# Setup of a graph-attention kernel: the first eight loads ordered anew over two DMA queues, and three chunks of the neighbours' sums computed ahead of q's projection

## The chip, the cores and the metric

The kernel runs on one core of one Trainium2 chip. The metric is the device time of one execution in microseconds (us): 586.49 us in the median of three runs (586.25 to 587.98). The core's engines are named as the profile names them: PE is TensorE's matmul, PEld its weight load, DVE is VectorE, ACT is ScalarE, POOL is GpSimd, SP is SyncE, which here does nothing but issue transfers. A name with a q behind it (SPq, ACTq) is that engine's sequencer, from which a transfer (DMA) is issued.

## What is computed

One graph-attention layer over B = 16 graphs of N = 512 nodes with F = 512 features. Each node attends to the first NG = 20 nodes of its graph, in two directions d, with H = 16 heads of 32 features. Cut to what matters here:

```python
row_zero  = v.sum(-1) == 0                                  # (B, N)
q_exp     = where(row_zero, 0, q[:, None, :])               # q is (B, 512)
self_feat = concat([v, q_exp], -1) @ W_self.T + b_self      # (B, N, F)
output = self_feat
for d in range(2):
    A  = adj if d == 0 else swap(adj); A = A[:, :, :20, :]
    kv = self_feat[:, :20]
    qh, kh = self_feat @ Wq[d].T + bq[d], kv @ Wk[d].T + bk[d]
    aff = heads(qh) . heads(kh) / sqrt(32)
    aff = where(A.sum(-1) > 0, aff, NEG) + (A @ w_bias + b_bias)
    out_t = softmax(aff) @ kv                               # per head
    output += heads(out_t) @ Wout[d] + bout[d]
result = v + relu(output)
```

The first thing that all else needs is `self_feat` of the 20 neighbours of every graph, 16 * 20 = 320 columns: a product of their features with the first half of `W_self`, plus the product of q with the second half, the latter only where a node's features do not sum to zero.

## The kernel before, in words

The program is one function with its order of work written out by hand: each engine gets its instructions in the order in which the code names them, and waits where an operand isn't there yet. It has a setup (lines 458 to 764), in which the weights are loaded, the neighbours' features, keys and values are computed and the keys are folded into the score weights, and a loop over the 16 graphs (from line 786) with four tiles of 128 nodes each. The change touches the first 17 us of the setup alone.

Everything in the setup's beginning is cut into C = 4 chunks of 128 input features (the partitions):

- `xkv[:, k]`, 128 x 320, chunk k of the 320 neighbours' features (160 KB each); `ws_v[:, k]`, 128 x 512, chunk k of the half of `W_self` that multiplies them (256 KB each). The helper `kv_rows(k, queue)` (line 501) loads both: `xkv` always from SP's queue, `ws_v` from the queue given.
- `ws_q`, 128 x 4 x 512 (1024 KB), the half of `W_self` that multiplies q; `q_sb` (32 KB) is q itself.
- `bs_sb`, `bk_sb`: two small biases, needed by ACT at lines 579 and 592.

The loads stand at lines 506 to 528. ACT's queue issues `ws_v` chunks 0 and 1, `bs_sb`, `bk_sb`; SP's queue issues `xkv` chunks 0 and 1, `q_sb`, `ws_q`, then chunks 2 and 3 of `xkv` and `ws_v`, then the key weights `wk` (line 515, needed from line 586 on), the query weights `wq_sb`, a broadcast bias row, the first graph's `x` and so on.

The work on them, in PE's order:

1. seven matmuls on a tile of ones (line 496) that need no load;
2. `kv_terms(fc, k)` (line 536): for chunk k and each quarter fc of the output one fp32 matmul of 320 columns into the PSUM bank `kv_ps[fc]`; the profile shows each as two instructions. It runs for k = 0 and 1, that is 16 instructions;
3. q's projection (line 547): four matmuls into `ps_q`, one per chunk, eight instructions;
4. `kv_terms(fc, 2)`, eight instructions, while ACT copies q's projection from PSUM to `q4` (line 551);
5. the sum of the neighbours' features over all partitions (line 554, two instructions), from `rsk`, which POOL adds up from the four chunks of `xkv` (lines 531 to 533);
6. four matmuls of `q4` with a selecting matrix `sel` (line 559, eight instructions), which sum the four chunks' parts of q's projection and turn them; DVE copies the result to `qw` (line 563);
7. `kv_terms(fc, 3)`, eight instructions, beside which DVE and POOL form `qp`, DVE adds it to the finished bank (`kvn`, line 576) and ACT adds the bias (`kvT`, line 579);
8. `key_rows` (line 582), which needs `kvT` and `wk`, and from there the rest of the setup.

Of the kernel before, what the change touches and what calls it, by code (L numbers as in the profile page):

```python
# [13 lines left out]
P = 128  # L14
# [4 lines left out]
def gat_kernel(  # L19
# [20 lines left out]
    nc = tc.nc  # L40
    B, F, N = xT.shape
    NG, L = adj.shape[3], adj.shape[4]
    H, DH = 16, 32
    C = F // P
# [28 lines left out]
    ws_v = const.tile([P, C, F], F32, name="ws_v")  # L73
# [384 lines left out]
    with tc.tile_pool(name="setup", bufs=1) as sp, tc.tile_pool(name="ps_acc", bufs=4, space=PSUM) as acc["pool"]:  # L458
# [4 lines left out]
        q_sb = sp.tile([P, C, B], F32, name="q_sb")  # L463
# [10 lines left out]
        ws_q = load.tile([P, C, F], F32, tag="x", name="ws_q", bufs=3)  # L474
        wk_sb = [sfp.tile([P, C, F], F32, tag="sf", name=f"wk{d}") for d in range(2)]

        with tc.tile_pool(name="setup_k", bufs=1) as sk:
            xkv = sk.tile([P, C, BM], F32, name="xkv")
# [19 lines left out]
            def rows(sb, src, queue=nc.sync):  # L498
                queue.dma_start(sb, src.rearrange("(c p) f -> p c f", p=P))

            def kv_rows(k, queue=nc.sync):
                rows(xkv[:, k : k + 1], xkvT[bass.ts(k, P)])
                rows(ws_v[:, k : k + 1], wsT[bass.ts(k, P)], queue)


            kv_rows(0, nc.scalar)
            kv_rows(1, nc.scalar)
            nc.scalar.dma_start(bs_sb, b_self)
            nc.scalar.dma_start(bk_sb, bk)
            nc.sync.dma_start(q_sb, qT)  # L510
            rows(ws_q, wsT[F:])
            kv_rows(2)
            kv_rows(3)
            for d in range(2):
                rows(wk_sb[d], wkT[d])
            for d in range(2):
# [19 lines left out]
            def kv_terms(fc, k):  # L536
                nc.tensor.matmul(  # L537
                    kv_ps[fc][:, :BM], ws_v[:, k, bass.ts(fc, P)], xkv[:, k],
                    start=(k == 0), stop=(k == C - 1),
                )  # L540

            for k in range(2):
                for fc in range(C):
                    kv_terms(fc, k)

# [3 lines left out]
                )  # L549
            q4 = sk.tile([P, F], F32, name="q4")  # L550
            nc.scalar.copy(q4, ps_q[:, 0])
            for fc in range(C):
                kv_terms(fc, 2)
            nc.tensor.matmul(ps_q[:, 1, :BM], ones, rsk, start=True, stop=True)
            nc.vector.tensor_scalar(nzk, ps_q[:, 1, :BM], 0.0, None, ALU.not_equal)

# [510 lines left out]
```

## Time and profile before

| | |
|---|---|
| median of three runs | 586.49 us |
| the profiled execution's own time | 586.05 us |
| its span from the first to the last instruction | 583.9 us |
| PE busy | 575.7 us, 99% of the span |
| DVE busy | 489.0 us, 84% |
| ACT busy | 395.6 us, 68% |
| POOL busy | 384.9 us, 66% |
| moved by DMA | 124.14 MB, mean 213 GB/s |

The profile is one execution; its times are counted from the first instruction. A busy PE is not PE at its peak: a matmul's record is stretched by the one ahead of it, so starts are better evidence than ends. In a row of the timeline stand the start, the duration, the engine, the line, the operation, the tile written and those read, the count, and in brackets how long the engine was idle before and what released it. In a row on issues stand the tile and its source, the queue, the count, the size and the time from issue to landing. The chain of waits gives start, duration and name of each piece of the path that ended last.

### The profile page before, as it was taken

The numbers are of one execution on the slowest core, as the hardware profiler recorded it, in microseconds if no ns is written. First come the engines' busy times: TensorE is split into PE (matmuls) and PEld (weight loads), VectorE is DVE, ScalarE is ACT, GpSimd is POOL, SyncE is SP. The second block draws the span as 40 slices with busy tenths as digits, with TensorE's granted clock in tenths as the row PEclk, the third lists the DMA queues.
The fourth block names the chain that finished last, engine by engine and source line by source line (L and its number), as shares of the span: only waits on it lengthen the run. The fifth ranks groups of instructions, "written<-read, shape, count | busy, mean of one in ns | idle before, by whom it ended". The sixth has DMA issues, their size and how long they took to land.

```text
span 583.9 us, 30310 instructions
## 1 busy us (share of the span) xinstructions
PE 575.7 (99%) x13184; PEld 437.0 (75%) x13184; DVE 489.0 (84%) x783; ACT 395.6 (68%) x1162; POOL 384.9 (66%) x351
## 2 busy tenths in 40 slices
PE   9999999999999999999999999999999999999996
PEld 6654547887878787877878787787887878787873
DVE  0485565889898989899999999898989898989895
ACT  1334644586877777868686868687786877777671
POOL 2405663648778685858586777686868677776775
PEclk9999999999999999999999999999999999999999
DMA  8999899857766675757576767676676765664404
GB/s 303 388 407 311 331 377 320 273 123 213 209 197 196 185 214 169 217 167 217 168 214 171 214 171 212 177 199 188 199 202 187 199 198 172 199 199 114 144 15 146
DMA packets 103220, 124.14 MB, mean 213 GB/s; under 512 B 21712, under 2 KB 71920, under 8 KB 101040
## 3 DMA queue, kind: packets, MB, share of 16 engines
q1 hardware_dynamic: 101296, 119.79, 66.8%
q8 instruction: 104, 1.70, 1.3%
q0 software_dynamic: 672, 1.36, 1.0%
q10 hardware_dynamic: 1120, 1.06, 0.5%
q14 instruction: 28, 0.23, 0.2%
HBM read 82.30 MB, written 40.24 MB: 210 GB/s over the span
## 4 chain that ended last, share of the span: by engine, by line
PE 98%; DVE 0%; issue 0%; ACT 0%; DVEq 0%
PE ps_s L365 46%; PE ps_a L282 17%; PE ps_c L282 9%; PE ps_o L435 6%; PE ps_d L282 4%; PE ps_v L649 3%; PE ps_k L586 3%; PE ps_sf L205 2%; PE ps_kv L537 2%; PE ps_o L779 1%; PE ps_warm L496 1%; PE ps_nz L189 0%; PE ps_s L354 0%; PE ps_c L622 0%; PE ps_q L547 0%
## 5 line engine op out<-in xcount | busy, mean ns | idle before, releaser
L365 PEld LDWEIGHTS ps_s<-g,sf 128*32 128x32 f32 x8192 | 262.8, 110 | 20.9 <-issue 13.0
L365 PE MATMUL ps_s<-g,sf 128*32 128x152 f32 x8192 | 276.7, 293 | 0.5 <-ACT st L689 0.5
L337 ACT COPY both<-add 32x80 f32<-32x80 f32 x512 | 130.8, 256 | 53.8 <-DVE add L328 48.0
L417 POOL TENSOR_TENSOR s<-s,sm 128x640 f32<-128x640 f32 x63 | 80.4, 1276 | 94.2 <-DVE sm L416 68.2
L344 POOL TENSOR_TENSOR full<-cq,both 128x640 f32<-128x640 f32 x64 | 100.4, 1568 | 27.5 <-issue 21.3
L317 ACT ACTIVATE prod<-adj,wb_sb 128x80 f32<-128x80 int32 x330 | 112.4, 433 | 0.0
L392 ACT ACTIVATE s<-s 128x640 f32<-128x640 f32 x63 | 46.5, 738 | 64.1 <-DVE s L387 63.8
L449 POOL TENSOR_TENSOR o<-o,x 128x512 f32<-128x512 f32 x60 | 76.4, 1297 | 0.0
L379 DVE TENSOR_TENSOR full<-ps_s,full 128x608 f32<-128x608 f32 x63 | 48.8, 774 | 27.9 <-PE ps_s L365 22.6
L415 DVE TENSOR_REDUCE sm<-s 128x32 f32<-128x640 f32 x63 | 50.8, 806 | 9.5 <-ACT s L392 9.2
L282 PE MATMUL ps_a<-t,ws_s 128*32 128x246 f32 x960 | 55.4, 370 | 0.0
L383 DVE TENSOR_REDUCE ps_s<-full 128x32 f32<-128x640 f32 x63 | 52.2, 828 | 2.2
L424 DVE STREAM_TRANSPOSE wt<-s 128x640 f32<-128x640 f32 x63 | 52.7, 837 | 0.6 <-POOL s L417 0.6
L387 DVE TENSOR_TENSOR s<-full,ps_s 128x640 f32<-128x640 f32 x63 | 51.5, 817 | 1.1
L282 PEld LDWEIGHTS ps_a<-t,ws_s 128*32 128x32 f32 x960 | 31.6, 110 | 16.0
L328 DVE TENSOR_REDUCE add<-prod 128x80 f32<-128x960 f32 x32 | 36.8, 1150 | 6.2 <-ACT prod L317 4.4
L247 POOL TENSOR_TENSOR t<-x 128x492 f32<-128x492 f32 x30 | 34.6, 1153 | 9.5 <-DVE ps_s L383 5.4
L446 ACT ACTIVATE o<-o,bo 128x512 f32<-128x512 f32 x60 | 38.3, 713 | 0.6 <-DVE o L444 0.6
L435 PE MATMUL ps_o<-wt,vd 32*32 32x512 f32 (+5 forms) x816 | 36.7, 578 | 0.0
L444 DVE TENSOR_TENSOR o<-ps_o,sf 128x512 f32<-128x512 f32 x60 | 36.7, 668 | 0.0
L289 DVE SCALAR_TENSOR_TENSOR u<-nz,qw,ps_a 128x246 f32<-128x246 f32 x90 | 36.6, 448 | 0.0
L247 POOL TENSOR_TENSOR t<-x,t 128x492 f32<-128x492 f32 x30 | 34.5, 1150 | 2.3 <-DMA x<-in_xT 1.1
(239 smaller groups left out, 719.5 us busy)
## 6 DMA issues: line engine op xcount, KB each, us to landing
g_d<-st SPq DMA_DIRECT2D x16, 1064.0 KB, 5.9
g<-g_d SPq DMA_DIRECT2D x56, 304.0 KB, 3.6
out_T<-o SPq DMA_DIRECT2D x60, 256.0 KB, 3.3
x<-in_xT SPq DMA_DIRECT2D x56, 256.0 KB, 3.2
xn<-in_xn SPq DMA_DIRECT2D x52, 256.0 KB, 3.3
adj<-in_adj SPq DMA_DIRECT2D x56, 220.0 KB, 3.2
nz<-nz_d SPq DMA_DIRECT2D x14, 256.0 KB, 4.6
wk<-in_wkT SPq DMA_DIRECT2D x2, 1024.0 KB, 7.7
```

The source lines that it names most:

```text
L247: done["xsum"] = nc.gpsimd.tensor_sub(t, one, two)
L282: nc.tensor.matmul(to, lhs, x[:, k], start=start, stop=stop, skip_group_check=n != 2)
L317: nc.scalar.activation(p[:, :, l], a[:, :, l], AF.Identity, scale=wb_sb[:, l : l + 1])
L337: nc.scalar.copy(adds[b, h][bass.ts(a, R), :, g], add[r].rearrange("p (t m) -> p t m", t=2))
L344: done["full"] = nc.gpsimd.tensor_add(f, cqs[b].unsqueeze(1).to_broadcast(shape), adds[b, nt // 2][:, nt % 2].unsqueeze(2).to_broadcast(sh ...
L365: nc.tensor.matmul(to, sfs[b][:, k, bass.ds(nt * P + (2 * g + j) * R, R)], of, start=(onto is None and k == 0 and (whole or j == 0)), stop ...
L383: nc.vector.tensor_reduce(mx, f, AX.X, ALU.max)
L387: done["weigh"] = nc.vector.tensor_sub(s, f, mx.unsqueeze(3).to_broadcast(full))
L417: done["normal"] = nc.gpsimd.tensor_mul(s, s, sm.unsqueeze(3).to_broadcast(full))
L424: nc.vector.transpose(wts[b][:, nt], s.rearrange("p a h m -> p (a h m)"))
L435: nc.tensor.matmul(banks[a][bass.ds(at // 2 * DH, n * DH)].rearrange("p (t n) -> p t n", n=32), vd[r, bass.ds(at * DH, n * DH)], wt[r, :, ...
L449: nc.gpsimd.tensor_add(o[:, c], o[:, c], xs[b][:, c])
```

## The change

The eight transfers that come first are others, and the queues of some are changed:

| place | before | after |
|---|---|---|
| SP's queue | `xkv` 0, `xkv` 1, `q_sb`, `ws_q`, `xkv` 2, `ws_v` 2, `xkv` 3, `ws_v` 3, then `wk` | `xkv` 0, `xkv` 1 to 3 as one transfer of 480 KB, `ws_v` 2, `ws_v` 3, then `wk` |
| ACT's queue | `ws_v` 0, `ws_v` 1, `bs_sb`, `bk_sb` | `ws_v` 0, `ws_v` 1, `ws_q`, `q_sb`, `bs_sb`, `bk_sb` |

On PE, `kv_terms` runs for k = 0, 1 and 2 ahead of q's projection; between the projection and the sum of features (item 5) no chunk is left.

```diff
             kv_rows(0, nc.scalar)
-            kv_rows(1, nc.scalar)
+            rows(xkv[:, 1:], xkvT[P:])
+            rows(ws_v[:, 1:2], wsT[P : 2 * P], nc.scalar)
+            for k in (2, 3):
+                rows(ws_v[:, k : k + 1], wsT[bass.ts(k, P)])
+            rows(ws_q, wsT[F:], nc.scalar)
+            nc.scalar.dma_start(q_sb, qT)
             nc.scalar.dma_start(bs_sb, b_self)
             nc.scalar.dma_start(bk_sb, bk)
-            nc.sync.dma_start(q_sb, qT)
-            rows(ws_q, wsT[F:])
-            kv_rows(2)
-            kv_rows(3)
             for d in range(2):
                 rows(wk_sb[d], wkT[d])
...
-            for k in range(2):
+            for k in range(C - 1):
                 for fc in range(C):
                     kv_terms(fc, k)
...
             nc.scalar.copy(q4, ps_q[:, 0])
-            for fc in range(C):
-                kv_terms(fc, 2)
             nc.tensor.matmul(ps_q[:, 1, :BM], ones, rsk, start=True, stop=True)
```

## The prediction, made before the changed kernel ran

> **What bounds the kernel now.** I read the page first, then the chain of waits over the first 20 us, then the issues and the timeline of that stretch.
>
> ```profile
> span 583.9 us, 30310 instructions
> PE 98%; DVE 0%; issue 0%; ACT 0%; DVEq 0%
> ```
>
> PE carries 98% of the chain that ended last, so whatever moves PE's work in the setup moves the end by the same amount unless some later wait takes it up. The chain over the stretch that the change touches:
>
> ```profile
> 1.04 3.36 PE ps_warm L496 x14
> 4.40 5.49 PE ps_kv L537 x16
> 9.89 0.98 PE ps_q L547 x8
> 10.87 2.35 PE ps_kv L537 x8
> 13.22 0.54 PE ps_q L554 x2
> 13.76 0.80 PE ps_q L559 x8
> 14.56 2.25 PE ps_kv L537 x8
> 16.81 3.28 PE ps_k L586 x11
> ```
>
> Every piece begins where the last one ended. From 1.04 us on there is no hole: no transfer holds PE up, neither chunk 1 nor `ws_q`. What a new order could win by removing a wait is therefore close to nothing, and what it can lose is a wait that isn't there yet. The chain's times are ends of matmuls; the starts that I need below are in the timeline:
>
> ```profile
> 4.25 5.64 PE L537 MATMUL ps_kv<-xkv,ws_v 128*128 128x320 f32 x16
> 9.82 0.13 PEld L547 LDWEIGHTS ps_q<-ws_q,q_sb 128*16 128x16 f32 x8 [0.44 <-issue]
> 10.94 0.59 ACT L551 COPY q<-ps_q 128x512 f32<-128x512 f32 x1 [6.96 <-PE ps_q L547]
> 13.33 1.13 PEld L559 LDWEIGHTS ps_q<-sel,q 128*128 128x128 f32 x8
> 16.64 9.10 PE L586 MATMUL ps_k<-kvT,wk 128*128 128x320 f32 x32
> ```
>
> **When chunk 1 is needed.** The 16 instructions of chunks 0 and 1 don't run at one pace:
>
> ```profile
> 4.25:6.49 2.24, 2.24 (x4) 1.51 (x5) 1.00 1.02 334
> 10.80:12.95 2.15, 2.15 (x8) 1.44 (x8) 1.00 1.04 390
> ```
>
> The first number behind a stretch is its length, then PE's busy time and count, PEld's, the granted clock, the DMA engines' share and GB/s. Four instructions take 2.24 us at first, 0.56 each; later eight take 2.15 us, 0.27 each, though the granted clock reads 1.00 in both. So chunk 0 (eight instructions) ends its issue at 4.25 + 2.24 + 4 * 0.27 = 7.57 us, and chunk 1 is needed then; chunk 2 at 7.57 + 2.15 = 9.72, q's projection at 11.87.
>
> **When the loads land.** Issue times and times to landing (rows of issues whose window holds one transfer of each queue, in order of issue):
>
> ```profile
> 0.73 0.88 SPq L499 DMA_DIRECT2D xkv<-in_xkvT  x2
> 1.19 0.42 SPq L499 DMA_DIRECT2D xkv<-in_xkvT  x1
> 2.12 0.44 SPq L499 DMA_DIRECT2D ws_q<-in_wsT  x1
> 4.22 0.33 SPq L499 DMA_DIRECT2D xkv<-in_xkvT  x1
> ...
> xkv<-in_xkvT SPq DMA_DIRECT2D x1, 160.0 KB, 3.3
> ws_v<-in_wsT ACTq DMA_DIRECT2D x1, 256.0 KB, 3.5
> ...
> xkv<-in_xkvT SPq DMA_DIRECT2D x1, 160.0 KB, 4.0
> ws_v<-in_wsT ACTq DMA_DIRECT2D x1, 256.0 KB, 4.2
> ...
> ws_q<-in_wsT SPq DMA_DIRECT2D x1, 1024.0 KB, 7.0
> ```
>
> `xkv` 0 landed at 0.73 + 3.3 = 4.03, `xkv` 1 at 1.19 + 4.0 = 5.19; `ws_v` 0 and 1, issued beside them, 0.2 us behind each. The two queues advance row by row together: 128 rows of SP's for 128 rows of ACT's, although a row of `ws_v` is 1.6 times as long. One such pair takes 5.19 - 4.03 = 1.16 us. `ws_q` landed at 2.12 + 7.0 = 9.12, ahead of the 9.82 at which PE took it up: its slack is 0.70 us.
>
> **The change, part by part.**
>
> *Three chunks of `xkv` in one transfer.* PE's chunk 1 and POOL's first sum now wait for all 384 rows. By the pace above, with ACT's rows in between (`ws_v` 1, then `ws_q`), it lands at 4.03 + 3 * 1.16 = 7.51 us. Needed: 7.57. That is a tie; with some 0.05 us from a landing to the instruction that waits I count 0 to 0.1 us, and take 0.05. The ends: if SP's rows went alone, 480 KB at 334 GB/s take 1.47 us, it lands at 5.50 and nothing waits; if ACT's `ws_v` 1 and `ws_q` (1280 KB) went first, 1760 KB at 334 GB/s take 5.40 us, it lands at 9.43 and PE stands still for 1.9 us. I take the value between because the landings in pairs are the nearest rows. Queued behind a late chunk 1 on PE is everything.
>
> [...]
>
> *`ws_q` and `q_sb` on ACT's queue.* By pairs of 128 rows, `ws_v` 2 and 3 on SP's queue go beside the second half of `ws_q`, 512 KB a pair; at 390 GB/s that is 1.34 us, so both queues are done with the eight first transfers at 7.51 + 2 * 1.34 = 10.2 us (at 334 GB/s 10.7), `q_sb` a little behind, and `ws_v` 2 at about 8.9. All are later than before (`ws_q` by 1.1 us), and all early enough: 8.9 against 9.72, 10.2 to 10.7 against 11.87. Cost 0. If that cover of 1.1 us is gone, PE waits a microsecond for each microsecond.
>
> *PE's order.* The instructions are the same, so their sum stays. But chunk 2 stood between q's projection and the turn at line 559, and hid ACT's copy. In the chain the projection ends at 10.87; the copy runs from 10.94 to 11.53, that is until 0.66 us after it; chunk 2 covered 2.35 us. Now only line 554's 0.54 us lie between. Left over are 0.12 us, plus what the weight load of line 559 usually does ahead (13.33 against a piece that begins at 13.76) and now can't: I take 0.2 us in all, between 0.1 and the whole copy, 0.59. No gain is possible here. Behind it, the distance from line 559 to `key_rows` is the same on PE (chunk 3) and on DVE and ACT, so they shift together.
>
> *POOL's sums.* Three additions run when `xkv` is whole:
>
> ```profile
> 9.69 0.86 POOL L533 TENSOR_TENSOR rsk<-rsk,xkv 128x320 f32<-128x320 f32 x1 [3.50 <-DMA xkv<-in_xkvT]
> 10.77 0.86 POOL L533 TENSOR_TENSOR rsk<-rsk,xkv 128x320 f32<-128x320 f32 x1 [0.21 <-DMA xkv<-in_xkvT]
> ```
>
> From 7.51 on, 3 * 0.86 plus two gaps of 0.2 end at 10.5 us, before 11.63, and line 554 needs them at 11.87 + 0.98 = 12.85. Cost 0; cover 2.3 us.
>
> *The queues' issue.* A ninth transfer was held back until the first had landed: SP's third `xkv` at 4.22 stands in the waits as
>
> ```profile
> SPq L499 <- DMA ws_v<-in_wsT: 1.6, 1, 1.6
> SPq L499 <- DMA ws_q<-in_wsT: 2.4, 1, 2.4
> ```
>
> Now the ninth and tenth are `bs_sb` and `bk_sb` on ACT's queue, which holds ACT until the landing of `ws_v` 0 at 4.2 and one more issue of some 0.4 us; its next work for others is the copy at 11.87 + 0.98 + 0.07 = 12.9. `wk` comes eleventh and waits for the third transfer, so it is issued at 7.5 instead of 6.31. It doesn't matter as long as the queues have data:
>
> ```profile
> 5.00:10.00 5.00, 5.00 (x20) 3.17 (x22) 0.00 (x0) 0.00 (x0) 1.17 (x2) 1.00 1.01 342
> wk<-in_wkT SPq DMA_DIRECT2D x1, 1024.0 KB, 7.7
> ```
>
> The DMA engines are full (1.01), and the same 2726 KB stand ahead of `wk` before and after. So it lands at 6.31 + 7.7 = 14.0 us as before, give or take 0.4, and is needed at 16.6. All later transfers keep their order. Cost 0; two transfers fewer save SP some 0.8 us of issue that nobody waits for.
>
> **The sum.** 0.05 (chunk 1) + 0.2 (q4's copy) + 0 + 0 + 0 = 0.25 us more. Against the profiled execution's own 586.05 us this gives 586.30; the median of the three runs lies 0.44 us above that execution, and on it the sum gives 586.74. I predict 586.7 us: no change that can be measured, since about 0.3%, 1.76 us, is what a measurement of this kernel tells from none (its three runs span 1.73 us).
>
> **The rivals.**
>
> 1. *Chunk 1 is late* (slower). If ACT's queue gets ahead of SP's third transfer, PE stands still from 7.57 to as late as 9.43: +1.9, with the copy +2.1, time 588.6, slower by 0.36%. It decides from a landing of 9.1 us on (7.57 + 1.76 - 0.2). For it: `ws_q` is the longest transfer and now stands second behind `ws_v` 0. Against it: the even pairs. 8%.
>
> 2. *The pause brings the slow pace back* (slower). The slow matmuls of 4.25 to 6.49 follow 1.04 to 4.25 of short ones; if a pause at 7.57 starts that again, as long as from 1.04 to 6.49, half of 5.45 us is lost: 2.7, and with 0.25 the time is 589.4. Against it: there is a tie, not a pause of microseconds. 4%. [...]
>
> 3. *The stream of loads gets shorter* (faster). Eight large transfers are in flight from the start. The first 5 us show what there is to gain:
>
> ```profile
> 0.00:5.00 5.00, 3.96 (x16) 3.62 (x17) 0.92 (x3) 1.28 (x1) 1.35 (x10) 1.00 0.65 189
> ```
>
> The engines were 65% busy, but the rest is the start itself. Even if the loads came 0.5 us sooner, PE's chain has no DMA in it, so 586.5 to 586.0 is the end of it. To pass -1.76 us it would have to be worth 1.76 us of PE's idle time, and in the setup there is 1.04 us, before the first matmul. 6% for a gain of that size from something I don't see.
>
> 4. *The change doesn't do what it says.* q's weights on a queue of their own don't arrive earlier (10.2 instead of 9.1), and no one waited for them; nothing is gained, and the copy of q4 is uncovered. This is my forecast. With a wait on chunk 1 of up to 1.4 us it stays within the bound. 82%.
>
> **How the numbers follow.** Forecast 82%, of which the time is 586.5 to 587.4 on the median and, with the scatter of the runs (from 586.25 to 587.98), 585.6 to 588.3; rivals 1 and 2 lie above, 12%; rival 3 below, 6%. The range reaches from 585.6 to 588.6, which takes in rival 1's end and leaves out rival 2, rival 3's large gain and some scatter. Faster 0.06, same 0.81, slower 0.13, the last a little above rivals 1 and 2 because the terms of the sum all point up.
>
> **What would show it.** Right: the chain of the changed kernel has 24 instructions of line 537 in one piece from 4.40 on to about 12.0, with a first start at 4.25; the one transfer of `xkv` lands 7.0 to 7.9 us from the start; ACT's copy begins near 13.0; before line 559's weight load an idle time on ACT's copy of 0.1 to 0.4 us; `key_rows` begins at 16.8 to 17.0 instead of 16.64. Wrong: PE idle on `xkv` for over 1 us, matmuls of line 537 at 0.56 us after 7.5, a `ws_q` that lands after 11.9, or `key_rows` before 16.5; and if `key_rows` begins as forecast and the time differs by over 1 us, the cause lies behind the setup, where I expect nothing.

## The result, and the profile after

The changed kernel takes 588.57 us in the median of 14 runs (587.29 to 591.89), the kernel before 586.58 us in 14 runs beside them (585.96 to 588.47): a ratio of 1.0038, 95% interval 1.0021 to 1.0054. It is slower, by some 2 us, where no measurable change was forecast. The profiled execution took 587.86 us, its span is 585.7 us against 583.9.

The chain of waits over the first 20 us of the changed kernel (start, duration, what):

```profile
4.46 7.97 DMA q_sb<-in_qT
...
12.52 1.09 PE ps_q L548 x8
...
13.62 0.59 ACT q L552
...
14.36 0.78 PE ps_q L553 x2
15.13 0.80 PE ps_q L558 x8
15.93 2.25 PE ps_kv L538 x8
```

Before, this stretch was PE alone. Now a transfer of 32 KB, `q_sb`, and ACT's copy of q's projection stand in it. The same in the list of what PE waited for in the whole execution of the changed kernel:

```profile
PE ps_q L553 <- ACT q L552: 0.8, 1, 0.8
PE ps_d L282 <- issue: 0.7, 1, 0.7
PE ps_q L548 <- DMA q_sb<-in_qT: 0.7, 1, 0.7
```

The wait at line 282, some 110 us from the start, was there before with the same 0.7 us; the other two are new. PE's timeline gives the starts:

```profile
8.69 3.12 PE L538 MATMUL ps_kv<-xkv,ws_v 128*128 128x320 f32 x11
12.52 1.05 PE L548 MATMUL ps_q<-ws_q,q_sb 128*16 128x512 f32 x8 [0.71 <-DMA q_sb<-in_qT]
14.36 0.78 PE L553 MATMUL ps_q<-rsk,ones 128*128 128x320 f32 x2 [0.79 <-ACT q L552]
14.97 0.96 PE L558 MATMUL ps_q<-sel,q 128*128 128x16 f32 x8
```

The projection and the turn in the kernel before:

```profile
9.82 1.05 PE L547 MATMUL ps_q<-ws_q,q_sb 128*16 128x512 f32 x8
13.60 0.96 PE L559 MATMUL ps_q<-sel,q 128*128 128x16 f32 x8
```

The turn (line 558, before 559) starts at 14.97 instead of 13.60 us, 1.37 us later. The distance from q's projection to the turn is 14.97 - 12.52 = 2.45 us; before it was 13.60 - 9.82 = 3.78, of which chunk 2's eight instructions at 0.27 took 2.15, so 1.63 without them: 0.82 us more. The projection itself starts 0.55 us later than the 9.82 + 2.15 = 11.97 us at which it would have started before with chunk 2 ahead of it. PE's later instructions carry the shift to the end: the span is 1.8 us longer.

The changed kernel's issues (start and duration of the issuing), ACT's and then `wk` on SP's queue; below them, in order of issue, the size of a transfer and the time from its issue to its landing:

```profile
0.73 0.90 ACTq L499 DMA_DIRECT2D ws_v<-in_wsT  x2
1.66 0.50 ACTq L499 DMA_DIRECT2D ws_q<-in_wsT  x1
4.46 0.34 ACTq L512 DMA_DIRECT2D q_sb<-in_qT  x1
4.83 0.44 ACTq L513 DMA_DIRECT2D bs_sb<-in_b_self  x1
...
2.65 3.82 SPq L499 DMA_DIRECT2D wk<-in_wkT  x2
```

```profile
xkv<-in_xkvT SPq DMA_DIRECT2D x1, 480.0 KB, 5.2
ws_v<-in_wsT ACTq DMA_DIRECT2D x1, 256.0 KB, 4.9
...
ws_q<-in_wsT ACTq DMA_DIRECT2D x1, 1024.0 KB, 9.9
ws_v<-in_wsT SPq DMA_DIRECT2D x1, 256.0 KB, 6.2
...
ws_v<-in_wsT SPq DMA_DIRECT2D x1, 256.0 KB, 7.0
...
wk<-in_wkT SPq DMA_DIRECT2D x1, 1024.0 KB, 10.8
...
q_sb<-in_qT ACTq DMA_DIRECT2D x1, 32.0 KB, 8.0
...
bs_sb<-in_b_self ACTq DMA_DIRECT2D x1, 2.0 KB, 8.5
```

`xkv` 1 to 3, issued at 1.19, landed at 6.4 us, `ws_v` 1 beside it at 6.1; `ws_v` 2 and 3, issued at 1.65 and 2.2, landed at 7.9 and 9.2; `ws_q` at 1.66 + 9.9 = 11.6; `q_sb` at 4.46 + 8.0 = 12.5, and `bs_sb` at 13.3. PE had finished three chunks at 11.65 (the last of the 11 instructions above starts 10 * 0.27 us after 8.69, and takes 0.27).

One thing no single profile shows: the runs fall into two groups. Nine of the 14 have a mean granted clock of 0.996 to 0.999 and a median of 588.3 us; five have 0.991 to 0.993 and a median of 590.7 us. Of the kernel before, 98 runs beside the experiments below have a listed clock, and none of them is under 0.996.

### The profile page after: what moved, and what is told of

The parts are those of the page before. It is cut to its first block, busy times and chain, and to the rows that moved or that the text cites. A ratio compares the mean times of both kernels' runs of the same rounds, so it can differ in the third digit from the quotient of the medians.

```text
span 585.7 us, 30303 instructions
## 1 busy us (share of the span) xinstructions
PE 575.8 (98%) x13184; PEld 436.6 (75%) x13184; DVE 488.2 (83%) x783; ACT 395.6 (68%) x1162; POOL 384.7 (66%) x351
## 4 chain that ended last, share of the span: by engine, by line
PE 96%; DMA 2%; ACT 0%; issue 0%; DVE 0%; DVEq 0%
PE ps_s L365 46%; PE ps_a L282 17%; PE ps_c L282 9%; PE ps_o L435 6%; PE ps_d L282 4%; PE ps_v L648 3%; PE ps_k L585 3%; PE ps_sf L205 2%; DMA q_sb<-in_qT 1%; PE ps_o L778 1%; DMA ws_v<-in_wsT 1%; PE ps_kv L538 0%; PE ps_nz L189 0%; PE ps_s L354 0%; PE ps_c L621 0%
```

## The experiments

Theory A: the cost has three terms. `q_sb` lands late, since it stands behind `ws_q` on ACT's queue and `wk` shares the DMA engines with that; ACT's copy is no longer covered, and already line 553's sum waits for it; and the holes that both leave in PE's work make the clock halve in some runs. The rivals, B to J, are named with the runs. Times are medians, each beside the kernel before on the same chip.

| run | edit | us | before, us | difference | ratio, 95% interval | runs with clock under 0.995 |
|---|---|---|---|---|---|---|
| e5_after_again | none | 587.97 | 586.80 | +1.17 | 1.0035 (1.0016 to 1.0055) | 3 of 12 |
| e1_q_first | `q_sb` ahead of `ws_q` | 588.28 | 587.26 | +1.02 | 1.0004 (0.9987 to 1.0020) | 0 of 12 |
| e2_loads_only | PE's order of before | 591.36 | 587.26 | +4.10 | 1.0064 (1.0039 to 1.0088) | 3 of 6 |
| e3_order_only | loads of before | 589.92 | 587.26 | +2.66 | 1.0052 (1.0032 to 1.0072) | 3 of 12 |
| e4_filled | short matmuls in the holes | 589.07 | 587.26 | +1.81 | 1.0026 (1.0010 to 1.0041) | 0 of 12 |
| e6_sum_apart | sum in the tile `ps` | 588.61 | 586.80 | +1.81 | 1.0022 (1.0010 to 1.0035) | 1 of 12 |
| e7_both | e1 and e6 | 587.38 | 586.80 | +0.58 | 1.0012 (1.0003 to 1.0022) | 0 of 12 |
| e8_loads_filled | e2 with its pause filled | 590.82 | 586.80 | +4.02 | 1.0064 (1.0046 to 1.0081) | 0 of 6 |
| e9_tiles_swapped | e1, tiles of sum and turn exchanged | 586.23 | 586.65 | -0.42 | 0.9995 (0.9986 to 1.0005) | 0 of 11 |
| e10_wq_split | e1, `ws_q` halved over both queues | 586.36 | 586.65 | -0.29 | 0.9996 (0.9983 to 1.0008) | 0 of 12 |
| e11_split_swapped | e9 and e10 | 586.12 | 586.65 | -0.53 | 0.9992 (0.9981 to 1.0002) | 0 of 11 |
| e12_q_last | `q_sb` behind the small biases | 593.25 | 586.63 | +6.62 | 1.0091 (1.0062 to 1.0121) | 4 of 6 |

The difference of medians and the ratio, which weighs all the runs, don't agree to the tenth where the runs fall into two groups or the kernel before scatters, as beside e1 to e4 (586.18 to 590.43 us).

**The changed kernel again.**

> The changed kernel once more, beside the next three on one chip. Theory A (late q_sb, uncovered copy, and a clock that halves in some runs): 1.2 to 2.0 us over the kernel before; q_sb lands 0.7 to 0.9 us after ws_q; a wait of 0.7 to 0.9 us on the copy ahead of line 553's sum; some runs with a mean clock under 0.995. Rival E (the low clocks belonged to the chip of the first comparison alone): no run under 0.995.

It came out nearly so: +1.17 us, just under A's 1.2, and three of 12 runs at a clock of 0.991 or 0.992. Rival E in this form falls: the low clocks come on this chip, and in e3 below on another.

The new profile also shows how much the setup differs between executions of one kernel. The records of the three chunks' 24 instructions end at 12.44 us here and at 11.81 in the first profile, and PE's idle time ahead of the projection shrank from 0.71 to 0.19 us. In e9 and e4 below they end at 10.93 and 11.08 us. A difference of a few tenths between two profiled setups is therefore no evidence by itself.

**`q_sb` first.**

```diff
+            nc.scalar.dma_start(q_sb, qT)
             rows(ws_q, wsT[F:], nc.scalar)
-            nc.scalar.dma_start(q_sb, qT)
```

> The changed kernel with q_sb (32 KB) issued on ACT's queue ahead of ws_q instead of behind it. Theory A (three terms: q_sb lands late behind ws_q, the copy of q's projection is uncovered, and in some runs the clock halves after the holes): q_sb lands at about 7 us, ws_q at 11.6 to 12.0, q's projection starts at 11.7 to 12.1 instead of 12.52, the turn at line 558 0.4 to 0.8 us earlier than 14.97; time 587.7 to 588.2, 0.4 to 0.8 us under the changed kernel. Rival B (it is ws_q that is late, q_sb only lands near it): projection still at 12.4 or later, time as the changed kernel, 588.6.

```profile
12.20 1.05 PE L548 MATMUL ps_q<-ws_q,q_sb 128*16 128x512 f32 x8
14.04 0.78 PE L553 MATMUL ps_q<-rsk,ones 128*128 128x320 f32 x2 [0.79 <-ACT q L552]
...
q_sb<-in_qT ACTq DMA_DIRECT2D x1, 32.0 KB, 5.8
...
ws_q<-in_wsT ACTq DMA_DIRECT2D x1, 1024.0 KB, 9.9
```

`q_sb` lands at 7.5 us (issued at 1.66), but `ws_q`, issued at 2.19, now lands at 12.1, half a microsecond later than in the changed kernel. The projection starts at 12.20, 0.3 us earlier and not 0.4 to 0.8. So A and B both have a part: behind the late `q_sb` stands a late `ws_q`. (In this execution PE had its three chunks done only at some 11.9 us, 10.59 + 5 * 0.27, so this profile alone shows little waiting for `ws_q`; e9's, with 1.38 us of it, does.) No run has a low clock.

**Loads alone and order alone.**

```diff
-            for k in range(C - 1):
+            for k in range(2):
...
             nc.scalar.copy(q4, ps_q[:, 0])
+            for fc in range(C):
+                kv_terms(fc, 2)
```

> The loads of the changed kernel with PE's order of before (two chunks, q's projection, chunk 2, the rest). Theory A: chunk 1 ends at about 9.3 us, PE stands still until q_sb lands at 12.4, so 3 us; the copy is covered again; line 559's turn starts at about 16.2 instead of 13.60, key_rows 2.6 us later than before; time 589.2, and more where the clock halves after the 3 us pause, up to 592. Rival C (the loads cost nothing, the cost is PE's order alone): 586.6, as before.

PE's wait for `q_sb`, its timeline and its windows in that run (length, PE busy and count, PEld, DVE, ACT, POOL, clock, DMA share, GB/s):

```profile
8.72 0.43 PE L538 MATMUL ps_kv<-xkv,ws_v 128*128 128x320 f32 x1
12.73 1.91 PE L548 MATMUL ps_q<-ws_q,q_sb 128*16 128x512 f32 x8 [3.57 <-DMA q_sb<-in_qT]
...
4.36:11.18 6.82, 4.61 (x17) 2.96 (x16) 0.00 (x0) 1.28 (x1) 2.57 (x3) 1.00 1.05 396
11.19:18.00 6.81, 5.27 (x15) 2.44 (x16) 0.00 (x0) 0.58 (x1) 0.00 (x0) 0.50 1.06 382
18.01:25.00 6.99, 6.99 (x31) 4.70 (x30) 3.18 (x7) 2.42 (x5) 2.48 (x4) 1.00 1.06 392
```

PE pauses from 9.15 to 12.73, and from 11.2 to 18.0 us the granted clock is 0.50: the projection's eight instructions take 1.91 us instead of 1.05. Rival C falls: the new loads cost more with the old order than with the new one, and this difference is the worst but one of all.

The order alone is the converse edit on the kernel before:

> The loads of before with PE's order of the changed kernel (three chunks ahead of q's projection). Theory A: chunk 2's weights land at 10.23 us where 9.72 would be needed, a wait of 0.5 us; q_sb and ws_q are there; the uncovered copy costs 0.86 us as in the changed kernel, because line 554's matmul waits for the copy too; the turn at 14.9 to 15.0 instead of 13.60; time 587.9 to 588.1. Rival as the prediction had it (copy 0.2 us): 587.2 to 587.4. Rival D (PE's order costs nothing, the loads are all of it): 586.6.

```profile
PE ps_kv L537 <- DMA ws_v<-in_wsT: 1.7, 1, 1.7
...
PE ps_q L552 <- ACT q L551: 0.8, 1, 0.8
```

The copy's 0.8 us is as expected, so rival D falls, and the prediction's 0.2 us too. The wait for chunk 2 is 1.7 us, not 0.5: in this run `ws_v` 2 landed at 11.0 us instead of 10.2, and PE was ready earlier. Hence 2.66 us over before, where some 1.4 was expected.

**The holes filled.** Four matmuls on ones, put twice into the changed kernel, and 15 of them into e2's pause:

```diff
...
+            for _ in range(4):
+                nc.tensor.matmul(ps[:, 1, 2 * P : 3 * P], ones, ones, start=True, stop=True)
             for k in range(C):
                 nc.tensor.matmul(
                     ps_q[bass.ds(k * DH, B), 0], q_sb[:, k], ws_q[:, k], start=True, stop=True
```

> The changed kernel with four short matmuls on the tile of ones (0.86 us) put into each of PE's two holes, ahead of q's projection and ahead of line 553's sum; their results are never read. Theory A (the runs over 589.5 us, 5 of 14, whose mean granted clock is 0.991 to 0.993, are those in which the holes made the clock halve): the holes are filled, all runs have a clock of 0.995 or more, none is over 589.5, median 588.2 to 588.6. Rival E (these runs have nothing to do with the holes): about a third of the runs still at 0.991 to 0.993 and over 589.5.

> The loads of the changed kernel with PE's order of before, as the run that took 591.4 us, and with 15 short matmuls on the tile of ones (3.2 us) in the pause ahead of q's projection; their results are never read. Theory A (of that run's 4.1 us over before some 1.5 to 2.5 are the clock that halved from 11.2 to 18.0 us because PE paused): the pause of some 3 us is as long, the clock stays at 1.00 through 11 to 18 us, chunk 2 takes 2.35 us instead of 4.04; time 2.3 to 3.0 us over before, 1.5 us or more under that run. Rival H (the clock halves whatever PE does there): as that run, 4 us over before.

On the clock both say the same. None of e4's 12 runs is under 0.996, where the changed kernel had 8 of 26 at 0.991 to 0.993 in its two comparisons (it was not run unfilled on e4's chip); e8's six are at 0.997 to 0.999, e2's six at 0.993 to 0.996. So rivals E and H fall as to the clock. On the time the two runs say little. Four of e4's runs are over 589.5 us in spite of their clock, where A expected none, and in its profile 0.5 us of the first hole was left. e8 missed its 2.3 to 3.0 us and took the 4.0 of rival H, though not with a halved clock: the short matmuls ran too long, and the loop's first matmuls waited longer (the release isn't shown):

```profile
10.08 3.51 PE L549 MATMUL ps_q<-ones 128*128 128x128 f32 x30
13.52 1.05 PE L551 MATMUL ps_q<-ws_q,q_sb 128*16 128x512 f32 x8
14.51 2.42 PE L538 MATMUL ps_kv<-xkv,ws_v 128*128 128x320 f32 x8
16.76 0.70 PE L558 MATMUL ps_q<-rsk,ones 128*128 128x320 f32 x2
...
PE ps_a L282 <- issue: 2.1, 1, 2.1
```

The short matmuls end at 13.5 us; in e2, with the same loads, `q_sb` was there at 12.6. Chunk 2 takes 2.25 us from start to start (14.51 to 16.76), so the slow pace is gone. What the halved clock costs by itself is therefore read from e2's and e12's profiles, not from e8's time.

**The sum's tile.**

```diff
-            nc.tensor.matmul(ps_q[:, 1, :BM], ones, rsk, start=True, stop=True)
-            nc.vector.tensor_scalar(nzk, ps_q[:, 1, :BM], 0.0, None, ALU.not_equal)
-
             ps = ps_s.tile([P, 2, 512], F32, tag="s", name="ps_q")
+            nc.tensor.matmul(ps[:, 1, P : P + BM], ones, rsk, start=True, stop=True)
+            nc.vector.tensor_scalar(nzk, ps[:, 1, P : P + BM], 0.0, None, ALU.not_equal)
```

> The changed kernel with line 553's sum written into the second PSUM tile, ps, instead of the unused bank of ps_q, which ACT is reading. Theory A (the sum waits for ACT's copy only because both are in the tile ps_q): the sum starts 0.52 us after the last matmul of q's projection instead of 1.38, the copy's uncovered part falls from 0.86 to 0.2 to 0.35 us, the turn and key_rows come 0.5 to 0.65 us earlier than in the changed kernel, and so does the end. Rival F (the sum waits for something else, rsk for example, or the turn behind it waits as long): no gain, 0 to 0.1 us.

```profile
12.33 1.05 PE L548 MATMUL ps_q<-ws_q,q_sb 128*16 128x512 f32 x8 [0.18 <-issue]
13.31 0.81 PE L554 MATMUL ps_q<-rsk,ones 128*128 128x320 f32 x2
14.79 0.37 PE L558 MATMUL ps_q<-sel,q 128*128 128x16 f32 x2 [0.68 <-DVE nzk L555]
```

The sum no longer waits, but the turn does, for DVE's reading of the sum in the tile that the turn writes: 2.46 us from the projection to the turn, as in the changed kernel. No gain, as rival F said, and by A's own mechanism in another place.

> Both mendings: q_sb ahead of ws_q on ACT's queue, and the sum in the tile ps. Theory A (the two terms add): 0.3 to 0.5 us from q_sb and 0.5 to 0.65 from the sum, so 0.8 to 1.15 us under the changed kernel and 0.2 to 0.6 us over the kernel before; the rest is the late ws_q (11.6 to 12.1 us) and what is left of the copy. Rival G (the rest is the loads' order as such, farther back): over 1.2 us above the kernel before still.

It came out at +0.58 us, at the upper end of A's range over before, and 0.59 us under the changed kernel, less than A's 0.8: the projection at 12.40 and the turn at 14.86 us leave the sum's gain out, as in e6.

**The tiles exchanged, and `ws_q` on both queues.** In e9 the sum goes into `ps` and the turn into `ps_q`, whose readers are done by then; in e10 the loads are, with the tiles as in the changed kernel:

```diff
-            for k in (2, 3):
-                rows(ws_v[:, k : k + 1], wsT[bass.ts(k, P)])
-            rows(ws_q, wsT[F:], nc.scalar)
+            rows(ws_v[:, 2:3], wsT[2 * P : 3 * P])
             nc.scalar.dma_start(q_sb, qT)
+            rows(ws_q[:, :2], wsT[F : F + 2 * P], nc.scalar)
+            rows(ws_q[:, 2:], wsT[F + 2 * P :])
+            rows(ws_v[:, 3:4], wsT[3 * P : F])
```

> q_sb ahead of ws_q, the sum written into the tile ps and the turn into the tile ps_q, whose readers are done by then. Theory A (a matmul waits for any reader of its whole tile; e6_sum_apart only exchanged the wait for ACT's copy for one for DVE's reading of the sum): neither the sum nor the turn waits for DVE; the turn starts 1.7 to 2.0 us after the projection's first matmul instead of 2.45; with the projection at 12.2 to 12.4 the turn is at 14.0 to 14.3; 0.5 us under e7_both, 0.0 to 0.4 us over the kernel before. Rival G (the wait has another cause): 2.4 us again, and 0.6 us over the kernel before.

> The changed kernel with q_sb first on ACT's queue and ws_q in two halves, one on ACT's queue, one on SP's ahead of ws_v 3 and wk; tiles as in the changed kernel. Theory A (ws_q lands at 11.5 to 12.3 instead of the forecast 10.2 to 10.7 because wk stands beside it on SP's queue): both halves land by 10.8, the projection starts at 11.6 to 11.8 without a wait, the turn at 14.1 to 14.3, key_rows at 17.1 to 17.3; 0.5 to 0.9 us over the kernel before, all of it the copy. Rival J (ws_q is late because the DMA engines were slower than forecast): halves land at 11.5 or later, projection at 12.2 or later.

> ws_q in halves on both queues, q_sb first, and the tiles of the sum and the turn exchanged. Theory A (the three terms are all there is): projection at 11.6 to 11.8, turn 1.7 to 2.0 us later at 13.4 to 13.7, key_rows at 16.4 to 16.7; within 0.2 us of the kernel before, no run under a clock of 0.995. Rival G (something else of the change costs, farther back): 0.5 us or more over the kernel before.

PE's timeline in e9, then in e10 with the landing of the two halves (issued at 2.18 and 2.19):

```profile
12.31 1.05 PE L548 MATMUL ps_q<-ws_q,q_sb 128*16 128x512 f32 x8 [1.38 <-DMA ws_q<-in_wsT]
13.29 0.81 PE L554 MATMUL ps_q<-rsk,ones 128*128 128x320 f32 x2
14.05 1.06 PE L558 MATMUL ps_q<-sel,q 128*128 128x16 f32 x8
```

```profile
11.75 1.05 PE L549 MATMUL ps_q<-ws_q,q_sb 128*16 128x512 f32 x8
13.60 0.78 PE L554 MATMUL ps_q<-rsk,ones 128*128 128x320 f32 x2 [0.80 <-ACT q L553]
...
ws_q<-in_wsT SPq DMA_DIRECT2D x1, 512.0 KB, 7.3
ws_q<-in_wsT ACTq DMA_DIRECT2D x1, 512.0 KB, 7.6
```

In e9 the turn comes 1.74 us after the projection instead of 2.45: in the changed kernel (0.79 us) and in e6 (0.68) a matmul waited for the reader of its tile though it writes the tile's other columns, and with the tiles exchanged no reader is left. In e10 the halves land at 9.5 and 9.8 us, the projection starts at 11.75 without a wait: two chunks on each queue, ahead of `wk`, are through earlier than four on one (11.6 in the changed kernel), of which the last two had `wk` beside them. Rivals G and J fall.

The intervals of all three take in the kernel before: with both terms mended, and with either the late `ws_q` or the shared tile mended alone beside `q_sb`, nothing of the cost can be measured any more. That is better than A's own numbers for e9 and e10. In e10's profile the turn is at 14.2 us, 0.6 us behind the 13.60 of before, and the median doesn't show it; what the executions of the kernel before lose now and then (585.0 to 588.3 us on that chip) no profile here shows. The varying time of the first chunks, seen above in the changed kernels, may be a part of it. e11's ratio of 0.9992 (0.9981 to 1.0002) is the lowest, and not clear of 1. No version beats the kernel before by more than can be measured, which fits a PE without holes before.

**`q_sb` later still.**

```diff
-            nc.scalar.dma_start(q_sb, qT)
             nc.scalar.dma_start(bs_sb, b_self)
             nc.scalar.dma_start(bk_sb, bk)
+            nc.scalar.dma_start(q_sb, qT)
```

> The changed kernel with q_sb behind bs_sb and bk_sb on ACT's queue. Theory A (each small transfer behind ws_q lands 0.8 us after the one before it, PE waits for q_sb one for one, and the longer PE pauses between 11 and 15 us the oftener the clock halves): q_sb lands at 13.8 to 14.2, the projection starts 1.4 to 1.7 us later than in the changed kernel; more than a third of the runs have a mean clock under 0.995, and if the profiled one is among them its clock is 0.50 over some 6.8 us that begin between 11 and 15 us; time 3.0 to 5.5 us over the kernel before. Rival E (low clocks have nothing to do with PE's pause): time 2.8 to 3.4 us over, low clocks in no more than a third of the runs.

```profile
15.07 1.91 PE L548 MATMUL ps_q<-ws_q,q_sb 128*16 128x512 f32 x8 [3.80 <-DMA q_sb<-in_qT]
...
20.53 4.62 PE L538 MATMUL ps_kv<-xkv,ws_v 128*128 128x320 f32 x8
24.94 5.46 PE L585 MATMUL ps_k<-kvT,wk 128*128 128x320 f32 x19
...
11.30:14.70 3.40, 0.00 (x0) 0.00 (x0) 0.00 (x0) 0.00 (x0) 0.00 (x0) 1.00 1.07 384
14.70:18.10 3.40, 2.24 (x9) 0.54 (x10) 0.00 (x0) 0.59 (x1) 0.00 (x0) 0.55 1.05 387
18.10:21.60 3.50, 3.50 (x12) 2.85 (x12) 1.21 (x3) 0.00 (x0) 0.56 (x1) 0.50 1.05 387
21.60:25.00 3.40, 3.40 (x8) 2.08 (x7) 1.47 (x3) 1.41 (x3) 1.84 (x3) 0.50 1.06 401
25.40:28.00 2.60, 2.60 (x11) 1.89 (x10) 0.56 (x2) 0.84 (x2) 2.44 (x3) 1.00 1.06 385
```

The pause grew to 3.80 us and four of six runs have a low clock; in the profiled one it is halved for 10 us from about 15 us on, and eight instructions of chunk 3 take 4.4 us (20.53 to the next start at 24.94) instead of 2.24. That is more than expected in each number (`q_sb` landed at 15.0 us, 6.26 us plus 8.7; 6.6 us over before), in the direction of A and against E.

The low clocks can also be sorted by the holes between PE's matmuls that each run's profile has in the setup. With one hole of 0.7 to 1.4 us (e1, e7, e9, e10) none of 47 runs has a clock under 0.995. With two there are 3 of 12 in e3 (1.7 and 0.8 us), 1 of 12 in e6 (0.2 and 0.7) and 8 of 26 in the changed kernel (0.7 and 0.8, in e5's profile 0.2 and 0.8). What decides whether a hole counts, no run here shows.

## Why the prediction was wrong

The forecast was 586.7 us and no change; 588.57 lies at the edge of its range, on the side of rivals 1 and 2. Step by step:

**Chunk 1** (0 to 0.1 us): right that it doesn't hold PE up; 24 instructions run in one piece. The landing was off: 6.4 us where 7.51 was worked out from rows that advance in pairs. `ws_v` 1 landed at 6.1, so the 384 rows of `xkv` passed beside the 128 of `ws_v` 1, and not beside 384 of ACT's. That rows of the two queues always go in pairs, no trace shows: in the kernel before, SP's queue moved 72 packets and ACT's 73 from 2.8 to 3.4 us, but 95 and 31 from 3.6 to 4.0; in the changed kernel it was 540 and 320 from 2.8 to 6.0, and 288 and 291 from 6.4 to 9.2. Chunk 0 began 0.23 us later (4.48) and yet the chunks ended at 11.65 instead of 11.87, since fewer of the first matmuls went at the slow pace (the first four took 1.78 us, before 2.24): a difference between executions that the sum didn't have.

**`ws_q` and `q_sb` on ACT's queue** (cost 0): this step failed. `ws_q` landed at 11.6 instead of 10.2 to 10.7, `q_sb` not a little but 0.9 us behind it. What was wrong is the count of pairs. I let half of `ws_q` pass beside `xkv` until 7.51 and the other half beside `ws_v` 2 and 3, in two pairs of 1.34 us. But `xkv` was through at 6.4 with `ws_v` 1 beside it, and all four chunks of `ws_q` were still to come: two beside `ws_v` 2 and 3, which landed at 7.9 and 9.2, so about 1.35 us a pair as forecast, and two beside `wk`. That makes 6.1 + 4 * 1.35 = 11.5 us, an estimate from these landings. The same count fits e10, where `q_sb` landed at 7.1 and the two chunks of `ws_q` behind it at 7.1 + 2 * 1.35 = 9.8. The early `xkv` and the late `ws_q` are thus one error. Why `xkv` got through so early is open: no run changes the first rows alone.

The queues' issue was misread too: I took `q_sb` as one of the eight transfers that need not wait and `wk` as the eleventh, issued at 7.5. In fact `wk`'s first half went out eighth, at 2.65 us, and `q_sb` ninth, at 4.46. But this didn't make `ws_q` late. In e1 `q_sb` was among the first eight (issued at 1.66), `wk` by the order of the code behind them, and `ws_q` landed at 12.1 all the same; on SP's queue `wk` comes after `ws_v` 3, which landed at 9.2, so an issue at 7.5 would hardly have kept it from `ws_q` either.

PE then waited for `q_sb` one for one, as the prediction said it would if the cover was gone. Cost: 0.77 us, which is the 0.87 from the end of three chunks (11.65) to the projection (12.52), less the 0.10 that this change of matmuls took before (16 instructions end at 7.57 + 2.15 = 9.72, the projection starts at 9.82). The chunks' earlier end gave 0.22 of it back, which makes the 0.55 us above.

**PE's order** (0.2 us, from 0.1 to 0.59): the mechanism was right, ACT's copy is uncovered, and the term was mis-sized: 0.82 us. I had line 554's sum run under the copy. It writes the other half of the tile that ACT reads, and waits for the whole copy (13.62 to 14.21; the sum starts at 14.36, after 0.79 us of idleness); so nothing covers it. The upper end was too low for that reason. e6, where the sum in another tile doesn't wait, and e9 show it.

**POOL's sums** (0): right; PE never waited for them.

**Rival 2** (4%): this is what happened in part. In 5 of 14 runs the mean clock is low, and these runs are about 2.4 us above the rest. The prediction tied it to a pause of microseconds; here two holes of 0.7 and 0.8 us within 3 us go with a low clock in 8 of 26 runs. In the changed kernel itself no profile caught a halved setup: that it is there as in e2 and e12 is inferred from the clocks, and from the filled holes that end them. The group moves the median little: the nine others have 588.3 us, still 1.7 over before. In e2, with one long hole, the clock fell 2.0 us into it (9.15 to 11.18); in e12 some 3.8 us (11.27 to about 15.0, an estimate from the window that begins at 14.70 with a mean of 0.55).

**Rival 4**, my forecast, was right in saying that q's weights on their own queue come later and nobody had waited for them; it priced the harm at 0.25 us, and the profile's setup shows 1.37. Some 0.4 us of the span's 1.8 lie behind the setup. About half of that has come up by the last group of line 435 in the chain, which starts at 574.51 us before and 576.13 after, 1.62 later; the rest lies behind it. What causes either stays open, as does what sets the wait at line 282, which lies between nothing (e9) and 2.1 us (e8).

## What to carry to other kernels

An engine without a hole in its chain can hardly gain from a new order of its loads: here PE had none from 1.04 us on in the stretch that was changed, and no version gained anything clear. Before moving one, list for each transfer what passes beside it on the other queue until it lands: here `xkv` was through at 6.4 us instead of 7.51, and `wk` came to pass beside the last two chunks of `ws_q`. Ask above all what becomes of a small transfer behind a large one: `q_sb`, 32 KB, landed 0.9 us behind `ws_q`. Work taken out from between a producer and its reader can uncover the latency (0.82 us here), and what is left there may wait for the same reader if it shares a tile with it (0.79 us in the changed kernel, 0.68 in e6). A hole in TensorE's work can have a second price, the clock, which one profile may not show: two holes of 0.7 and 0.8 us went with a low clock in 8 of 26 runs. Look at the clock of all runs.

## What the runs showed of the hardware that was not expected

- A small transfer behind a large one on a queue, with another queue full beside it, cost some 0.9 us in both sizes seen: in the changed kernel 32 KB, then 2 KB landed 0.9 us each after the one ahead (11.6, 12.5, 13.3 us). Both are 128 rows; from 11.6 to 12.5 us ACT's queue moved 176 packets and SP's 175, though ACT's were 0.01 MB and SP's 0.34.
- The granted clock reads 1.00 in the first microseconds of these profiles, though the first matmuls on loaded data run at the halved pace: 0.56 us each from 4.25 us on in the kernel before, 0.27 later, and 4.41 / 8 = 0.55 us in e12 where the column reads 0.50. In these profiles the column doesn't show that first slow stretch.
- Once halved, the clock stayed so for 6.8 us (e2, until 18.0) and 10 us (e12, until some 25.3), though PE was busy without a hole from 12.73 us on in e2 and from 17.77 in e12.
- Executions of one kernel differ in when the first chunks are done (the records of the same 24 matmul instructions end at 11.81 and 12.44 us in two profiles of the changed kernel), so the idle time behind them is long in one and short in the next (0.71 and 0.19 us).
